# Weights' tiles of the first pass in the experts' buffers, loads three products ahead, and the second layer's first head among attention's last pieces

## The chip, the cores and the metric

The kernel runs on one core of a Trainium2 chip. The metric is the time of one execution in device microseconds; a kernel's time is the median of several executions. All tensors are float32. Engines are named as in the profile: PE is TensorE's matmul, PEld its weight load, DVE is VectorE, ACT is ScalarE, POOL is GpSimd and SP is SyncE, which here only issues DMAs. "SPq" is SP's sequencer.

## The reference

Two transformer layers run over 8 x 256 tokens of 512 channels. The reference, cut to what is computed:

```
x = hidden_states                      # 8 x 256 x 512
xn = layernorm(x)
x = x + attention0(xn) + ffn0(xn)      # layer 1
xn = layernorm(x)
x = x + attention1(xn) + ffn1(xn)      # layer 2

attention0: q, k, v = silu(xn @ qkv_w.T)             # 32 heads of 128
            o  = decayed causal linear attention of q, k, v
            o  = norm_w * o * rsqrt(mean(o*o) + eps) # over all heads
            return sigmoid(xn @ gate_w.T) * o @ out_w.T
ffn0:       16 experts, top 2 of them (inner size 128), and a shared expert
attention1: one head of 128: softmax(q k.T / sqrt(128)) v @ Wo + bo
ffn1:       G = softmax of the top 16 of 64 scores;  h[n,k,r] = xn @ A
            return 2 * sum over k, r of (h * G) * B  # rank 16
```

## The kernel before

**Attention of layer 1** takes most of the time. Its projections are made with the seven-product scheme of Strassen and Winograd, at two levels. The outer level cuts the tokens and a head group's weights in quarters, which gives seven weights' products, taken in the `ORDER` p1, p2, p6, p5, p3, p7, p4. The inner level cuts each of those again in seven, which run as `Outer`'s steps p1, p7, (the preceding product's p3), p6, p4, p2, p5 (L728, into the PSUM banks ps_a, ps_e, ps_b). The list `plan` holds 224 products: 2 passes over the tokens (`i`), 8 head groups (`g`), 2 halves (`h`: q and k, then gate and v), 7 weights' products. A "unit" in this document is one head group of one pass: two halves, 14 products.

**Weights** (`weights`, L664 to 714). A weights' tile holds eight blocks of 128x256: four blocks of the outer product's weight and four inner sums. In the first pass, p1, p2 and p4 (`RAW`) load 512 KB. p5, p6 and p7 load two raw quarters, 512 KB each, and DVE makes their outer sum in two instructions of 128x512 (`outer_sum`). p6 loads a third quarter into a buffer `st` and subtracts it, ACT copies p6's finished sum into `st` (L1051), and p3 subtracts `st` from its one quarter. Three of the inner sums are made by DVE and one by POOL (`inner_sum`, all recorded on line L103). ACT's queue then stores the sums in `ws`, from which the second pass loads them.

**Buffers.** `big` is a ring of four 1 MB tiles for weights, and later for other things of that size. `staged` is a pair of buffers, used by `st`, by the experts' tiles `xw` (second pass only), and by `spare8`. `toks` has three buffers for the tokens' operands `xt` (896 KB each, loaded at L423).

**The order of the work.** While product n runs, `prepare(n + 2)` makes the product two ahead: it issues its weights' load, and its sums are put among the products' steps (`following.step`). Smaller pieces of work wait in a list: `later(after, f)` queues a piece and `slot()`, called after each of the inner products, runs the next one due. Scores (L840), attended values (L852), the gated result gT (L872) and the output projection (L925, into ps_sc) are such pieces, as are the 36 experts, which run in the second pass. PE, DVE and SP are ordered by a scheduler within the limits of data and of `tc.keep_in_program_order`; ACT and POOL run in program order.

**Around the join of the layers.** `low_sums` (twice, near the end of the second pass) makes with POOL the sums of the operands `fa` and `fb` of ffn1 and stores them in `low` by SP (L1207; loads at L1211 and L1233). When a pass's attention is complete, `settle_sums` adds up each chunk's products: POOL combines them, DVE makes r (`finish`, L654), SP stores it in `xs`. `wrapped_up` loads chunk 0's sum, adds the experts' outputs and normalizes it. Then attention ends, the pool `toks` is closed (`layer1.close()`), and layer 2 loads its operands (`operands`, L1397 to 1402). It runs four chunks of 512 tokens: `Head` (values and routing scores L1441, `choose`'s gates L1446 to L1467, q and k L1430 and L1475, scores L1483, softmax), then the low-rank products (L1552 with A's operands `WA`, L1649 with B's operands `XB`), with the head of the next chunk beside the last of them. The gates go through DRAM (`gd`) and come back spread over partitions (`spread_g`, L1523).

Of the kernel before, what the change touches and what calls it, by code (L numbers as in the profile page):

```python
# [73 lines left out]
def block_kernel(  # L74
# [35 lines left out]
    layer1 = ExitStack()  # L110
    toks = layer1.enter_context(tc.tile_pool(name="toks", bufs=3))
# [307 lines left out]
    first_w = []  # L419
# [53 lines left out]
    for i in range(NCH):  # L473
# [8 lines left out]
        if i == 1:  # L482
            for p in ORDER[0:2]:
                w = big("w")
                nc.sync.dma_start(out=w[:, 0:4], in_=w_att[0, 0, RAW[p]])
                first_w.append(w)
# [121 lines left out]

    all_rms = {}
# [48 lines left out]

    def spare8():
        return staged("spare")[:, 0 : TPC * C].rearrange("p (t c) -> p t c", t=TPC)  # L660

    with tc.tile_pool(name="attn", bufs=1) as attn, tc.manual_schedule(engines={mybir.EngineType.Activation, mybir.EngineType.Pool}):
        sums_ = {}
        previous = {}  # L664
        finished = []

        def weights(i, g, h, p, steps):

            loaded = len(first_w) > 0
            w = first_w.pop(0) if loaded else big("w")  # L670
# [3 lines left out]
            kept = ws[2 * g + h][p]  # L674

            if i == 0:
                if not loaded:
                    tc.keep_in_program_order(nc.sync.dma_start(out=y, in_=w_att[g, h, dict(RAW, p6=2, p5=2, p3=1, p7=0)[p]]))
                outer = []
                if p in ("p6", "p5", "p7"):  # L680
                    tc.keep_in_program_order(nc.sync.dma_start(out=w[:, 4:8], in_=w_att[g, h, 2 if p == "p7" else 3]))
                    outer = [(sub if p == "p7" else add, w[:, 4:8])]
                if p == "p6":
                    previous["s2"] = staged("st")[:, 0 : 4 * S].rearrange("p (b n) -> p b n", b=4)
                    tc.keep_in_program_order(nc.sync.dma_start(out=previous["s2"], in_=w_att[g, h, 0]))
                    outer.append((sub, previous["s2"]))
                if p == "p3":
                    outer = [(sub, previous["s2"])]

                def outer_sum(n):  # L690
                    for f, other in outer:
                        f(y[:, n : n + 2], y[:, n : n + 2], other[:, n : n + 2], v)
# [9 lines left out]
                if outer:  # L702
                    steps += [("p4", partial(outer_sum, 0)), ("p2", partial(outer_sum, 2))]
                if p == "p6":
                    steps += [("p5", partial(nc.scalar.copy, previous["s2"], y))]
# [5 lines left out]
            elif p in RAW:  # L711
                tc.keep_in_program_order(nc.sync.dma_start(out=w[:, 1:4], in_=w_att[g, h, RAW[p]][:, 1:4]))
                tc.keep_in_program_order(nc.sync.dma_start(out=w[:, 4:8], in_=kept))
            else:
                tc.keep_in_program_order(nc.sync.dma_start(out=w[:, 1:8], in_=kept))
# [482 lines left out]
        def low_sums(n):  # L1198
# [7 lines left out]
            def store(at, t):  # L1206
                nc.sync.dma_start(out=low[n][:, at], in_=t)  # L1207
# [19 lines left out]
            def sums3():  # L1227
                if n == 0:
                    sub(t0[:, 1], t1[:, 1], t1[:, 0], pool)
                else:  # L1230
                    sub(t0[:, 1], t0[:, 1], t1[:, 1], pool)
                store(2, t0[:, 1])
                nc.sync.dma_start(out=t1[:, 0], in_=f[:, 1])  # L1233
# [9 lines left out]
        def wrapped_up():  # L1243

            x_, y = spare8(), spare8()
            nc.sync.dma_start(out=x_, in_=xs_[0])
# [25 lines left out]

        def prepare(n):
            if n < len(plan):
                outers.append(make(n))
            elif n == len(plan):
                nonlocal wsm
                wsm = big("wsm").rearrange("p b n -> p (b n)")
                load_small(wsm)
            else:  # L1280
                nonlocal yT0
                yT0 = big("yT0").rearrange("p (c b) n -> p c (b n)", c=NC)
                for t in range(TPC):
                    later(1 + 2 * t, lambda t=t: turn_rows(yT0, settled[0], t, ps_sc()))

        wsm = yT0 = None
        outers = [make(0), make(1)]
        for n, (i, g, h, p) in enumerate(plan):
# [4 lines left out]
            if k == 0:  # L1293
# [15 lines left out]
                if at == 2 * NB * NG - 2:  # L1309
                    later(1, wrapped_up)  # L1310
# [25 lines left out]
        outers[-1].p3()  # L1336
        while pieces:
            slot()
# [43 lines left out]
    layer1.close()  # L1382
    work = ctx.enter_context(tc.tile_pool(name="work2", bufs=2))
    wob = work.tile([P, 2, C], FP, tag="wob", name="wob", bufs=1)
# [3 lines left out]
    wqkv_t, bv_t, bqk_t = (small_part(wsm, n) for n in ("wqkv", "bv", "bqk"))  # L1388
# [16 lines left out]
    wa = operands(0, fa, "fa")  # L1405
    WA = dict(zip(("p1", "p2", "p4", "p7", "p5", "p6", "p3"), wa))
    xb = operands(1, fb, "fb")
    XB = dict(zip(("p1", "p2", "p3", "p7", "p5", "p6", "p4"), xb))
# [4 lines left out]
    def next_x(i):  # L1413
        x_ = spare8() if i % 2 == 0 else big(f"x{i}").rearrange("p (t b) n -> p t (b n)", t=TPC)
# [5 lines left out]
    scale = 1.0 / float(P) ** 0.5  # L1420
    out_t = out.rearrange("(i t p) c -> i t p c", t=TPC, p=P)
    class Head:


        def __init__(self, i):
            self.i, self.yT = i, xT[i]

        def project1(self, pm, w, lo):
            for c in range(NC):
                mm(pm, w[:, c, lo : lo + P], self.yT[:, c, :], start=(c == 0), stop=(c == NC - 1))  # L1430

        def route(self):

            self.v = work.tile([P, TPC, P], FP, tag="v", name="v1", bufs=1)
            sc = work.tile([P, TPC, K], FP, tag="sc", name="sc64", bufs=1)
            n = P + K
            for h in range(2):
                pv = ps_sc()
                for t in range(2 * h, 2 * h + 2):
                    for c in range(NC):  # L1440
                        mm(  # L1441
                            pv[:, bass.ts(t % 2, n)], self.yT[:, c, bass.ts(t, P)], wqkv_t[:, c, 2 * P :],
                            start=(c == 0), stop=(c == NC - 1),
                        )
                pv = pv[:, 0 : 2 * n].rearrange("p (t d) -> p t d", t=2)
                nc.vector.tensor_copy(sc[:, bass.ts(h, 2), :], pv[:, :, P:])  # L1446
                tt(self.v[:, bass.ts(h, 2), :], pv[:, :, 0:P], bv_t.to_broadcast([P, 2, P]), ALU.add)
            self.G = work.tile([P, TPC, K], FP, tag="gate", name="G", bufs=1)
            for t in range(TPC):
                top = work.tile([P, 8], FP, tag="top", name="top")  # L1450
                rest = work.tile([P, K], FP, tag="rest", name="rest")
                top2 = work.tile([P, 8], FP, tag="top2", name="top2")
                rest2 = work.tile([P, K], FP, tag="rest2", name="rest2")
                nm = work.tile([P, 1], FP, tag="nm", name="nm")
                es = work.tile([P, K], FP, tag="es", name="es")
                tot = work.tile([P, 1], FP, tag="tot", name="tot")
                nc.vector.max(top, sc[:, t, :])
                nc.vector.match_replace(rest, top, sc[:, t, :], NEVER)
                nc.vector.max(top2, rest)
                nc.vector.match_replace(rest2, top2, rest, NEVER)  # L1460
                nc.vector.tensor_scalar(nm, top[:, 0:1], -1.0, None, ALU.mult)
                nc.scalar.activation(es, sc[:, t, :], AF.Exp, bias=nm)
                nc.vector.scalar_tensor_tensor(
                    self.G[:, t, :], rest2, NEVER, es, ALU.is_equal, ALU.mult, accum_out=tot
                )
                nc.vector.reciprocal(tot, tot)
                nc.vector.tensor_scalar(self.G[:, t, :], self.G[:, t, :], tot, SCALING, ALU.mult, ALU.mult)  # L1467

        def qk(self):
            self.q = work.tile([P, CH], FP, tag="q", name="q1", bufs=1)  # L1470
            self.k = work.tile([P, CH], FP, tag="k", name="k1", bufs=1)
            for n, o in enumerate((self.q, self.k)):
                pm = ps_sc()
                self.project1(pm, wqkv_t, n * P)
                nc.scalar.activation(o, pm, AF.Identity, bias=bqk_t[:, n : n + 1])  # L1475

        def softmax(self):

            self.probs = []
            for b in range(2):  # L1480
                p = ps_sc()
                for t in range(2):
                    mm(  # L1483
                        p[:, bass.ts(t, S)], self.q[:, bass.ts(2 * b + t, P)], self.k[:, bass.ts(b, S)],
                        start=True, stop=True,
                    )
                pb = work.tile([P, 2, S], FP, tag="S", name="pb")
                top = work.tile([P, 2], FP, tag="stop", name="stop")
                tot = work.tile([P, 2], FP, tag="stot", name="stot")
# [270 lines left out]
```

## Time and profile before

| | us |
|---|---|
| median of 3 runs | 2806.41 |
| their lowest and highest | 2805.08, 2815.6 |
| the profiled execution's own time | 2803.46 |
| its span, first to last instruction | 2801.8 |
| busy in the span: PE, DVE, POOL, ACT | 2660.6, 1840.5, 1673.3, 973.8 |
| mean granted TensorE clock | 0.990 |

By place in the span, in us from its start: up to about 190 the first layer norm, routing and operands' sums; from there to about 1250 attention's first pass; from there to 2481 its second pass, with the experts; from 2481.0 (the first instruction of L1441) layer 2, with chunk 1's values at 2565.7 and the later chunks' at 2637.5 and 2709.9.

The profile is of one execution. A line of instructions gives the source line, the engine, the operation, the tiles by name as out<-in, shapes and a count, then busy time and the mean of one in nanoseconds, then idle time of the engine before them and what released it. A line of waits gives the engine and line that wait, an arrow to what they wait for, and then the sum in us, the number of waits and the longest. In brackets on a timeline stands the idle time before an instruction and its releaser.

### The profile page before, as it was taken

The page shows a single profiled execution, that of the slowest core. Times are in us where ns is not written, and L with a number is a line of the kernel's source. Part 1 is how long each engine was busy: PE and PEld are TensorE (multiplying, and loading weights), DVE is VectorE, ACT ScalarE, POOL GpSimd, SP SyncE. Part 2 cuts the span into 40 slices and gives each one's busy share as a digit, 9 for nine tenths or more (in the row PEclk, how much of TensorE's full clock was granted, in tenths as well). Part 3 has the DMA queues.
Part 4 walks back from the last instruction along what each step waited for, and adds up shares of the span by engine and source line. Part 5 has one row for each costly group of instructions (what it writes and reads, how often), then busy time and mean ns, then how long its engine had stood idle before and what let it go on. Part 6 is the DMA issues. An engine that isn't in the chain of part 4 may idle for free. (4 is left out here: it accounts for less than half of the span.)

```text
span 2801.8 us, 39316 instructions
## 1 busy us (share of the span) xinstructions
PE 2660.6 (95%) x14218; PEld 2297.3 (82%) x14218; DVE 1840.5 (66%) x3017; ACT 973.8 (35%) x1472; POOL 1673.3 (60%) x1484
## 2 busy tenths in 40 slices
PE   8989999899999999999999999999999999979999
PEld 5478888788887888888888888898989888957877
DVE  8688697979797878774535455555545455666663
ACT  4334343433343433343343324242323343521221
POOL 7367676767676767666755656565556666562210
PEclk9999999999999999999999999999999999989999
DMA  6898777868686868695768677776767586543211
GB/s 248 304 358 292 249 274 242 292 220 305 223 308 211 314 217 311 213 340 207 257 227 309 230 268 256 255 262 233 280 220 287 204 344 216 201 168 125 78 47 62
DMA packets 167011, 676.61 MB, mean 241 GB/s; under 512 B 20208, under 2 KB 22768, under 8 KB 164208
## 3 DMA queue, kind: packets, MB, share of 16 engines
q1 hardware_dynamic: 131264, 525.38, 53.3%
q10 hardware_dynamic: 21024, 92.81, 8.3%
q0 software_dynamic: 14528, 55.88, 6.3%
q8 instruction: 115, 1.88, 0.3%
q14 instruction: 80, 0.66, 0.1%
HBM read 531.00 MB, written 145.87 MB: 242 GB/s over the span
## 5 line engine op out<-in xcount | busy, mean ns | idle before, releaser
L728 PE MATMUL ps_a<-xt,w 128*128 128x256 f32 x2688 | 720.8, 383 | 35.1 <-DVE c L103 23.9
L103 POOL TENSOR_TENSOR c<-c,r 128x512 f32<-128x512 f32 x320 | 443.1, 1407 | 218.3 <-DVE r L103 214.7
L103 POOL TENSOR_TENSOR c<-c 128x512 f32<-128x512 f32 x288 | 372.7, 1315 | 323.1 <-DVE c L103 316.3
L728 PEld LDWEIGHTS ps_a<-xt,w 128*128 128x128 f32 x2688 | 469.1, 191 | 99.7 <-issue 22.2
L1055 ACT COPY cp<-ps_a 128x512 f32<-128x512 f32 x448 | 261.3, 584 | 747.8 <-PE ps_a L728 613.9
L925 PE MATMUL ps_sc<-wo,gT 128*128 128x256 f32 x1792 | 424.8, 381 | 19.4 <-DVE gT L872 18.7
L103 DVE TENSOR_TENSOR w<-w 128x256 f32<-128x256 f32 (+1 forms) x432 | 350.3, 827 | 106.7 <-DMA w<-in_w_att_dram 83.5
L728 PE MATMUL ps_e<-xt,w 128*128 128x256 f32 x1344 | 369.7, 383 | 21.3 <-DVE c L103 12.1
L925 PEld LDWEIGHTS ps_sc<-wo,gT 128*128 128x128 f32 x1792 | 332.8, 190 | 68.2 <-DVE gT L872 24.6
L103 POOL TENSOR_TENSOR sums<-sums,sq 128x256 f32<-128x256 f32 x240 | 192.0, 800 | 180.4 <-ACT sq L863 170.4
L728 PEld LDWEIGHTS ps_a<-w,xt 128*128 128x128 f32 x1792 | 271.0, 191 | 23.2
L728 PEld LDWEIGHTS ps_e<-xt,w 128*128 128x128 f32 x1344 | 233.2, 192 | 55.4 <-DVE c L103 14.5
L728 PE MATMUL ps_a<-w,xt 128*128 128x128 f32 x1792 | 272.6, 275 | 0.0
L103 DVE TENSOR_TENSOR acc<-ps_sc,acc 128x512 f32<-128x512 f32 x196 | 133.5, 686 | 146.9 <-PE ps_sc L925 145.0
L872 DVE SCALAR_TENSOR_TENSOR gT<-ps_o,nw,c 128x256 f32<-128x256 f32 x256 | 111.6, 477 | 167.6 <-ACT sq L863 160.4
L1055 ACT COPY cp<-ps_e 128x512 f32<-128x512 f32 x224 | 131.1, 585 | 155.1 <-PE ps_e L728 154.5
L728 PE MATMUL ps_b<-xt,w 128*128 128x256 f32 x672 | 182.2, 380 | 0.0
L103 POOL TENSOR_TENSOR gT<-gT 128x512 f32<-128x512 f32 x128 | 164.3, 1284 | 28.7 <-DVE gT L872 26.2
L103 DVE TENSOR_TENSOR s<-ps_sc,decay 128x384 f32<-128x384 f32 x256 | 139.8, 549 | 51.7 <-PE ps_sc L840 50.1
L103 DVE TENSOR_TENSOR c<-ps_a,c 128x512 f32<-128x512 f32 x160 | 109.5, 685 | 84.7 <-PE ps_a L728 76.5
L852 PE MATMUL ps_o<-s,c 128*128 128x256 f32 x512 | 154.9, 384 | 10.4 <-DVE gT L872 10.3
L863 ACT ACTIVATE sq<-ps_o 128x512 f32<-128x512 f32 x128 | 76.4, 597 | 253.2 <-PE ps_o L853 252.3
(291 smaller groups left out, 4398.4 us busy)
## 6 DMA issues: line engine op xcount, KB each, us to landing
xt<-xc SPq DMA_DIRECT2D x224, 896.0 KB
w<-in_w_att_dram SPq DMA_DIRECT2D x160, 512.0 KB
w<-in_w_att_dram SPq DMA_DIRECT2D x48, 384.0 KB
wo<-in_w_out_dram SPq DMA_DIRECT2D x56, 256.0 KB
decay<-dec SPq DMA_DIRECT2D x32, 384.0 KB
yd<-ye SPq DMA_DIRECT2D x36, 256.0 KB
st<-in_w_att_dram SPq DMA_DIRECT2D x16, 512.0 KB
wos<-wo ACTq DMA_DIRECT2D x32, 256.0 KB
```

The lines of the kernel that those rows point to most:

```text
L103: (eng or nc.vector).tensor_tensor(o, a, b, op)
L728: mm(o, a, b, start=(first and ty == 0), stop=True, skip_group_check=True)
L852: mm(po[:, bass.ts(hh, S)], v[:, 0:P], s[:, 0:S], start=True, stop=False)
L863: nc.scalar.activation(sq, po, AF.Square)
L872: nc.vector.scalar_tensor_tensor(gT[:, h, :], po[:, bass.ts(h, S)], nw[:, n : n + 1], self.c[:, 2 * h + t, 0:S], ALU.mult, ALU.mult,)
L925: mm(py[:, bass.ts(t, S)], self.O[l, p][:, hh, bass.ts(t, P)], self.wo[p][:, hh, :], start=(t == 0 and hh == 0), stop=(hh == 1), skip_grou ...
L1055: nc.scalar.copy(c, bank)
```

## The change

It has three parts, all in one diff.

1. **First pass, weights.** `load_weights` and `load_ahead` issue the loads three products ahead. The tiles of p5 and p7 lie in `staged`. p6 and p5 are loaded together, one quarter for p6 and two for p5. p5's outer sum w5 is made with p6's (w5 + its second quarter, then w5 - y for p6), p3 subtracts p6's sum itself; `st`, its load and ACT's copy are gone.
2. **Low sums.** The stores and one load of `low_sums` are issued from POOL's queue, the three first loads still from SP's. `wrapped_up` is queued 14 steps later in place of 1.
3. **Join.** The pool `toks` is kept. Nine of the fourteen 256 KB chunks of A's operands go to its three buffers during the last products (`load_part`), the other five after. The first head is made in pieces among attention's last ones, with its tiles in a `big` buffer. B's operands are loaded within chunk 0 (`load_fb`), and `next_x` exchanges its two kinds of buffers.

```diff
-    layer1 = ExitStack()
-    toks = layer1.enter_context(tc.tile_pool(name="toks", bufs=3))
+    toks = ctx.enter_context(tc.tile_pool(name="toks", bufs=3))
...
+    def load_part(n):
+
+        t = toks.tile([P, 7, S], FP, tag="X", name="fa")
+        load_fa(t.rearrange("p b n -> p (b n)")[:, 0 : 3 * C].rearrange("p (c k) -> p c k", c=3), 3 * n, 3 * n + 3)
...
+        def load_weights(i, g, h, p):
+
+            if i or p not in ("p5", "p7"):
+                w = big("w")
+            else:
+                w = staged("w")[:, 0 : 8 * S].rearrange("p (b n) -> p b n", b=8)
+            kept = ws[2 * g + h][p]
...
+            if i == 0:
+                load(w[:, 0:4], w_att[g, h, dict(RAW, p6=0, p5=2, p3=1, p7=0)[p]])
+                if p in ("p5", "p7"):
+                    load(w[:, 4:8], w_att[g, h, 2 if p == "p7" else 3])
...
-                if outer:
-                    steps += [("p4", partial(outer_sum, 0)), ("p2", partial(outer_sum, 2))]
+                outer = []
                 if p == "p6":
-                    steps += [("p5", partial(nc.scalar.copy, previous["s2"], y))]
+                    w5 = loaded["p5"][0]
+                    outer = [(add, w5, w5, w5[:, 4:8]), (sub, y, w5, y)]
+                elif p == "p3":
+                    outer = [(sub, y, y, latest["p6"])]
+                elif p == "p7":
+                    outer = [(sub, y, y, w[:, 4:8])]
+                for n, when in ((0, "p4"), (2, "p2")):
+                    steps += [(when, partial(outer_sum, *at, n)) for at in outer]
...
             def store(at, t):
-                nc.sync.dma_start(out=low[n][:, at], in_=t)
+                pool.dma_start(out=low[n][:, at], in_=t)
...
-                nc.sync.dma_start(out=t1[:, 0], in_=f[:, 1])
+                pool.dma_start(out=t1[:, 0], in_=f[:, 1])
...
+        def load(n):
+            if n < len(plan):
+                i, g, h, p = plan[n]
+                for q in dict(p6=("p6", "p5"), p5=()).get(p, (p,)) if i == 0 else (p,):
+                    loaded[q].append(load_weights(i, g, h, q))
+
+        def load_ahead(n):
+            if n + 1 < len(plan) and plan[n + 1][0] == 0:
+                load(n + 1)
+            elif n < len(plan) and plan[n][0]:
+                load(n)
+
         def prepare(n):
+            load_ahead(n)
             if n < len(plan):
                 outers.append(make(n))
             elif n == len(plan):
...
+                load_part(0)
             else:
-                nonlocal yT0
+                nonlocal yT0, head
+                load_part(1)
...
+                for n in range(2):
+                    later((10, 12)[n], partial(head.valued, n))
+                    later((14, 16)[n], partial(head.qk_, n))
+                for t in range(TPC):
+                    later(13 + t, partial(head.choose, (t,), attn))
+                later(22, partial(head.gates, lambda: attn.tile([P, 512], FP, tag="sum", name="GT", bufs=4)))
...
+                later(20, softened)
...
                 if at == 2 * NB * NG - 2:
-                    later(1, wrapped_up)
+                    later(14, wrapped_up)
...
-    head = Head(0)
-    head.route()
-    head.qk()
-    head.softmax()
...
+        if i == 0:
+            fill1[5].append(load_fb)
```

## The prediction

> **What bounds the kernel now.** I start from the page, to see which engine is nearly full and what its clock is.
>
> ```profile
> span 2801.8 us, 39316 instructions
> PE 2660.6 (95%) x14218; PEld 2297.3 (82%) x14218; DVE 1840.5 (66%) x3017; ACT 973.8 (35%) x1472; POOL 1673.3 (60%) x1484
> PEclk9999999999999999999999999999999999989999
> ```
>
> TensorE is busy 95% of the span, so the change, which leaves its products alone, can only win idle time: 2801.8 - 2660.6 = 141 us, and a little lost clock. The windows tell where it lies: columns are the stretch and its length, then busy time of PE, PEld, DVE, ACT, POOL, the granted clock, DMA share and GB/s.
>
> ```profile
> 490.00:630.00 140.00, 129.41 (x701) 113.66 (x699) 115.97 (x165) 52.06 (x75) 95.38 (x88) 1.00 0.74 256
> 1500.00:1640.00 140.00, 139.98 (x819) 125.32 (x818) 70.01 (x116) 46.10 (x72) 83.09 (x76) 1.00 0.72 252
> 2200.00:2300.00 100.00, 94.95 (x524) 84.89 (x523) 47.77 (x76) 31.36 (x48) 66.37 (x50) 1.00 0.76 287
> 2481.00:2520.00 39.00, 21.57 (x76) 14.73 (x76) 32.32 (x70) 6.03 (x17) 29.81 (x25) 0.78 0.73 262
> ```
>
> The first pass (row one) leaves PE idle 10.6 us in 140, with DVE 83% busy; the second pass (row two) leaves it idle for nothing. Row three is where the low-rank operands' sums are made: 5 us lost. Row four is the join of the layers: 17.4 us idle and the clock at 0.78. Next, in the first pass (200 to 1250 us, where PE is idle 70 us in all), who waits for whom:
>
> ```profile
> DVE w L103 <- DMA w<-in_w_att_dram: 83.4, 44, 4.4
> DVE gT L872 <- ACT sq L863: 38.6, 21, 2.8
> ...
> PE ps_sc L925 <- DVE gT L872: 17.4, 19, 1.6
> PE ps_a L728 <- DVE c L103: 16.9, 24, 1.5
> PE ps_e L728 <- DVE c L103: 12.1, 8, 3.2
> PE ps_o L852 <- DVE gT L872: 9.1, 7, 2.5
> PE ps_e L728 <- DVE r L103: 8.1, 14, 1.7
> ```
>
> PE waits for DVE's results, and DVE stands 83.4 us before weights that have not landed. A wait of DVE costs only where it makes a result late: going through PE's gaps one by one, 48 of the 70 us have a DVE wait for a DMA (or issue) in the 18 us before them. The sums' durations in that stretch, by form (busy us, mean ns, idle before):
>
> ```profile
> L103 DVE TENSOR_TENSOR w<-w 128x256 f32<-128x256 f32 x309 | 239.4, 789 | 62.2 <-DMA w<-in_w_att_dram 51.6 <-issue 4.2 <-POOL sums L103 2.5
> L103 DVE TENSOR_TENSOR w<-w 128x512 f32<-128x512 f32 x89 | 89.3, 1023 | 36.9 <-DMA w<-in_w_att_dram 28.4 <-issue 5.6 <-POOL c L103 2.3
> L103 DVE TENSOR_TENSOR w<-w,st 128x512 f32<-128x512 f32 x60 | 79.7, 1346 | 11.6 <-DMA w<-in_w_att_dram 3.5 <-ACT st L1051 2.7 <-DMA wos<-wo 2.6
> ```
>
> Last, the join, on PE's timeline (start, length, idle before) and SP's queue:
>
> ```profile
> 2481.01 5.45 PE L1441 MATMUL ps_sc<-wsm,yT 128*128 128x192 f32 x32
> 2486.29 3.60 PE L1430 MATMUL ps_sc<-yT,wsm 128*128 128x512 f32 x8
> 2497.64 5.43 PE L1430 MATMUL ps_sc<-yT,wsm 128*128 128x512 f32 x8 [7.75 <-DVE v L103]
> 2514.04 2.50 PE L1483 MATMUL ps_sc<-k,q 128*128 128x256 f32 x5 [9.68 <-ACT k L1475]
> SPq L1207 <- POOL low L103: 41.6, 7, 10.9
> ```
>
> The head's projections wait behind four r operations of DVE (8.79 us, then 4.94) and a G of 5.69; SP stands 41.6 us for POOL's low sums with loads behind it.
>
> **Part 1: weights.** Per half of a head group, loads fall from 5.5 to 4.5 MB, DVE sums of 128x512 by two, and ACT's copy of p6's raw sum (1.04 us) goes. Over 16 halves: 16 MB less, 32 sums x 1.02 to 1.35 = 33 to 43 us of DVE, 16.7 us of ACT (35% busy: worth nothing by itself). DVE's are worth only what they make PE wait less.
>
> In the issue order of the changed kernel each weight load stands one product earlier on SP, in front of the token load of the product before it. A product lasts 144.6/14 = 10.3 us (a unit, two halves, repeats every 144.6 us), the longest wait is 4.4 us, and each load's slot is free by its turn. So the 83.4 us of waits should go almost whole. That moves the token loads (L423) behind one more 0.5 or 1 MB transfer, 2 to 4 us at 256 GB/s; SP stood 934.9 us for their slots, each fetched two products ahead, so I cost it at nothing; uncovered, it would cost those 2 to 4 us a product.
>
> What does that win? I laid DVE's work by product, from row durations, against PE's (130.1 us per unit in both kernels) in the issue order of each kernel, without DMA waits. DVE has 120.4 us per unit before and 116.3 after. Before, that order alone gives about 6.0 us of PE stalls per unit, 3.7 of them in p1 of the first half, where gT and the results c stand behind sums. The trace has 9.1, so the waits cost at least 3.1 x 8 units = 25 us; the gap count says at most 48. I take 35, nearer the lower, since a gap near a wait need not come from it.
>
> But the sums are bunched in the new order. With p5's tile loaded beside p6's, p6, p5 and already p7 have their sums ahead of p1's gT and c: DVE's weight work in that product rises from 7.1 to 12.3 us, and its whole work from 11.8 to 17.1, while PE has 10.4. Five later products fall by 2 to 4 us each. By the same hand lay p1's stalls grow from 3.7 to 5.5 or 7, 2 to 3.3 us per unit: taken 3, x 8 = 25. Ends: 0 (a queue ahead has slack), and 5.3 x 8 = 42 (nothing hides). First pass: 35 - 25 = 10 us won; ends 48 won and 42 - 25 = 17 lost.
>
> A rule against this: POOL works beside, and the 128x256 sum takes 789 ns in the mean where its shortest is 406. The Trainium skill, "SBUF — State Buffer", section "SBUF: two separate sides", says that a VectorE operation with two SBUF inputs and a GpSimd operation share a port pair as a lock, the loser blocked for the whole of the other. By the rule at its worst each of the some six sums pulled forward would wait out one POOL c of 1.41 us, 8.4 instead of 5.3 us per unit; the traced mean, which holds the average wait, is what the sum uses.
>
> **Part 2: low sums' DMAs on POOL's queue.** SP's waits at L1207 go; the three DMAs that POOL waits for landed 3.9 to 5.9 us late, and PE lost 5 us in that window. POOL, 66% busy there, issues 10 more DMAs, by the nearest row (indirect DMAs of POOL, about 1.06 us) 10.6 us in 100. I take 4 us won; ends 5 won, 5 lost (if combines behind those issues came late). "DMA: Bandwidth & Descriptors", section "Latency and other measured facts", has GpSimd's first byte about 0.4 us later than SP's; for ten DMAs that would be an estimated 4 us, no run shows it, and it would eat this gain only if each were waited for.
>
> **Part 3: the head among attention's last pieces.** PE's work stays (32 products of 128x192 at 5.45 us, two times eight at some 3.6 to 5.4, scores 2.5): it lengthens the tail as much as it shortens the join. Won are the two stalls, 7.75 + 9.68 = 17.4 us, and part of the clock (0.78 in 39 us with 21.6 busy: at most 4.7). What comes in their place: the r operations (8.79 + 4.94) still run on DVE, now ahead of low_rank's sums and copies; the operands of fa are in toks' slots before that, except the last five chunks (1.25 MB, 5 us at 262 GB/s); the loads of fb go behind the r stores on SP, which left at 2497 and 2506. XB's first product came at 2547 before, so 30 us remain. Chunk 0 takes 84.7 us to the next head (2481.0 to 2565.7) where later chunks repeat every 72, and the gaps after the two stalls (2.12, 2.58, 0.51 us) I leave as they are. I take 15 won; ends 22 won, and 8 lost if one r block (8.79) with fb behind it stands in front of PE.
>
> **Sum.** 2803.46 (the profiled execution: span 2801.8 and 1.7 around it) - 10 - 4 - 15 = 2774.5. The median of the runs, 2806.41, is 3 us higher: 2777.
>
> **Rivals.**
> (a) The waits were the whole of it: all 48 us go, the bunch hides in queues, and with 15 + 4 the time is 2806 - 67 = 2739. For it: no other engine is over 83% there, and DVE's work falls. Against: 22 us of gaps have no DMA wait near.
> (b) The stalls only change their name: what the waits cost the bunch costs again. 2806 - 19 = 2787. For it: the lay gives nearly the same per unit.
> (c) Slower: the bunch in p1 is paid in full, 5.3 us x 8 = 42, and the cure is nothing, as DVE's lag was from its order. 2806 + 42 - 19 = 2829. It decides from 19/8 = 2.4 us lost net per unit, the size I expect of the bunch before the cure. Against: three later products of PE (13.9, 14.3, 13.9 us) have 2 to 6 us more than DVE and absorb the lag.
> (d) The loads don't come earlier after all, since DMA is 74% busy; then 32 fewer sums win perhaps 5 us: 2782, inside the forecast's range. Against: 2 MB less per unit.
>
> **How the numbers follow.** My forecast (2762 to 2792) has 0.42, (a) 0.20, (b) with weaker joins up to 2806 0.20, (c) and milder forms of it 0.18. A measurement can tell this kernel from no change from about 0.5%, 14 us: below 2792 is faster, above 2820 slower. Faster: 0.42 + 0.18 from (a) + 0.04 of (b) = 0.64. Same: 0.16 of (b) + 0.02 of (a)'s chance, where the joins take the gain back, + 0.02 of (c) = 0.20. Slower: 0.16. The range runs from near (a), 2742, to 2822, past the milder half of (c), and leaves out about 2 in 10.
>
> **What would show it.** Right: DVE's wait for in_w_att_dram in the first pass from 83 to under 10 us; PE idle there from 70 to about 60, more before gT of p1; SP's wait for low gone and its window at 99%; the 7.75 and 9.68 gaps gone, XB's p1 some 15 us earlier. Wrong: DMA waits stay (d); PE ps_sc <- gT and ps_a <- c above 60 us together (c); PE idle below 30 us in the first pass (a); a new wait of PE for fa or fb.

## The result, and the profile after

The changed kernel takes 2839.49 us in the median (2837.77 to 2841.13), against 2807.51 us before: a ratio of 1.0109, 95% interval 1.0087 to 1.013. It is slower, where faster by 29 us was forecast. The page of the profiled execution shows both halves of it: DVE's work fell by 52 us (33 to 43 had been counted), and PE's busy time rose by 15 us, though it has the same 14218 products.

```profile
PE 2675.2 (94%) x14218; PEld 2315.7 (82%) x14218; DVE 1788.3 (63%) x2985; ACT 958.2 (34%) x1455; POOL 1662.2 (59%) x1494
```

The place is found with marks that both kernels pass: 200 us, the first expert's transposes (1364.59 before, 1401.44 after), and the values of chunk 1 in layer 2 (2565.70 and 2602.55). The windows between them, before first and then after (PE, PEld, DVE, ACT, POOL, the granted clock, DMA share, GB/s):

```profile
200.00:1364.59 1164.59, 1087.09 (x5896) 958.84 (x5894) 910.45 (x1309) 436.41 (x631) 790.56 (x697) 1.00 0.75 263
1364.59:2565.70 1201.11, 1167.16 (x6596) 1036.20 (x6597) 644.84 (x1041) 419.33 (x640) 719.68 (x630) 0.99 0.69 245
```

```profile
200.00:1401.44 1201.44, 1098.57 (x5905) 974.95 (x5905) 856.53 (x1276) 421.44 (x616) 773.42 (x702) 0.98 0.67 243
1401.44:2602.55 1201.11, 1169.51 (x6596) 1039.74 (x6597) 643.90 (x1040) 420.72 (x640) 727.46 (x640) 0.99 0.69 244
```

The first pass is 36.85 us longer. PE's idle time in it rose from 77.5 to 102.9 us (window less busy: 25.4 more), and its busy time by 11.5 us at a clock of 0.98 in place of 1.00. Two small parts of these belong elsewhere: 2.6 us of the idle time is PE's wait for the first expert's own tile (4.13 us before, 6.69 after, and 0.92 to 8.04 in the runs below), and the window after holds nine more recorded matmuls, an estimated 2 us of busy time. The second pass with the join has the same 1201.11 us in both: what parts 2 and 3 were to win is not there.

The waits of the first pass (200 to 1290 us), in total, number and longest:

```profile
DVE w L103 <- DMA w<-in_w_att_dram: 85.3, 37, 4.5
...
PE ps_o L996 <- DVE gT L1016: 26.4, 7, 4.0
...
PE ps_sc L1069 <- DVE gT L1016: 14.5, 7, 2.5
```

DVE still waits for weights as long as before (83.4 us), and PE now waits 40.9 us for gT in 14 long waits, two a unit, where it had 26.5 us in 26 shorter ones. DVE's timeline ahead of one of them, and PE's beside it:

```profile
562.08 2.36 DVE L103 TENSOR_TENSOR w<-w 128x512 f32<-128x512 f32 x2
564.36 0.68 DVE L103 TENSOR_TENSOR acc<-ps_sc,acc 128x512 f32<-128x512 f32 x1
564.96 5.57 DVE L103 TENSOR_TENSOR w<-w 128x512 f32<-128x512 f32 x7
570.45 0.86 DVE L1016 SCALAR_TENSOR_TENSOR gT<-ps_o,nw,c 128x256 f32<-128x256 f32 x2
```

```profile
571.46 0.68 PE L996 MATMUL ps_o<-s,c 128*128 128x256 f32 x2 [3.99 <-DVE gT L1016]
```

Nine weights' sums for coming products, 7.93 us, stand ahead of the gT that PE needs now; no DMA wait is among them. In the same place of the kernel before, three sums of 4.02 us stand there behind a DMA wait of 0.21, and PE waits 1.21:

```profile
550.57 2.81 DVE L103 TENSOR_TENSOR w<-w 128x512 f32<-128x512 f32 x2 [0.21 <-DMA w<-in_w_att_dram]
553.31 1.21 DVE L103 TENSOR_TENSOR w<-w,st 128x512 f32<-128x512 f32 x1
555.45 0.67 PE L852 MATMUL ps_o<-s,c 128*128 128x256 f32 x2 [1.21 <-DVE gT L872]
```

Times below are in us; each ratio compares with the kernel before on the same chip, and the interval is the 95% one.

### The profile page after: what moved, and what is told of

It reads as the page before. It is cut to its first block, busy times and chain, and to the rows that moved or that the text cites. A ratio compares the mean times of both kernels' runs of the same rounds, so it can differ in the third digit from the quotient of the medians.

```text
span 2839.4 us, 39099 instructions
## 1 busy us (share of the span) xinstructions
PE 2675.2 (94%) x14218; PEld 2315.7 (82%) x14218; DVE 1788.3 (63%) x2985; ACT 958.2 (34%) x1455; POOL 1662.2 (59%) x1494
## 5 line engine op out<-in xcount | busy, mean ns | idle before, releaser
L103 POOL TENSOR_TENSOR c<-c,r 128x512 f32<-128x512 f32 x320 | 449.9, 1428 | 218.1 <-DVE r L103 216.4
L103 POOL TENSOR_TENSOR c<-c 128x512 f32<-128x512 f32 x288 | 362.6, 1281 | 350.6 <-DVE c L103 341.6
L872 PEld LDWEIGHTS ps_a<-xt,w 128*128 128x128 f32 x2688 | 474.9, 193 | 86.0 <-issue 28.7
L1069 PE MATMUL ps_sc<-wo,gT 128*128 128x256 f32 x1792 | 427.4, 383 | 15.6 <-DVE gT L1016 14.5
L103 DVE TENSOR_TENSOR w<-w 128x256 f32<-128x256 f32 (+1 forms) x464 | 366.7, 823 | 119.4 <-DMA w<-in_w_att_dram 92.1
L103 POOL TENSOR_TENSOR sums<-sums,sq 128x256 f32<-128x256 f32 x240 | 185.6, 773 | 230.5 <-ACT sq L1007 220.4
L872 PE MATMUL ps_b<-xt,w 128*128 128x256 f32 x672 | 188.1, 390 | 0.0
L996 PE MATMUL ps_o<-s,c 128*128 128x256 f32 x512 | 157.3, 389 | 26.5 <-DVE gT L1016 26.4
L983 PE MATMUL ps_sc<-c 128*128 128x256 f32 x512 | 156.3, 387 | 17.4 <-DVE s L103 11.9
```

Source lines behind the costliest of these rows:

```text
L103: (eng or nc.vector).tensor_tensor(o, a, b, op)
L872: mm(o, a, b, start=(first and ty == 0), stop=True, skip_group_check=True)
L983: mm(p[:, 0:S], k[:, 0:P], q, start=True, stop=True)
L996: mm(po[:, bass.ts(hh, S)], v[:, 0:P], s[:, 0:S], start=True, stop=False)
L1069: mm(py[:, bass.ts(t, S)], self.O[l, p][:, hh, bass.ts(t, P)], self.wo[p][:, hh, :], start=(t == 0 and hh == 0), stop=(hh == 1), skip_grou ...
```

## Experiments: which part costs the time

**Everything but the weights.** The changed kernel with before's `weights` and loads:

```diff
-        def load_weights(i, g, h, p):
...
-            load_ahead(n)
```

> The changed kernel with the weights of the first pass as before (loads two ahead, st and ACT's copy, p5 and p7 in the ring); low sums on POOL's queue and the join stay changed. Theory (the loss lies in the first pass, in the order of DVE's sums): the first expert's transposes come at 1364 us again as before (1401 after), and the time is within 5 us of before, about 2806. Rival (the join or the low sums cost the 37 us): it stays near 2839.

Measured: 2807.99, ratio 0.9995 (0.9982 to 1.0008). All of the loss is in the weights' part. The first expert comes at 1370.42; its DVE waits 91.8 us for weights in the first pass, more than the 83.4 before and the 85.3 after, and it loses nothing by that against before. The sum of those waits says nothing of the time.

**Loads two ahead.**

```diff
-            if n + 1 < len(plan) and plan[n + 1][0] == 0:
-                load(n + 1)
-            elif n < len(plan) and plan[n][0]:
+            if n < len(plan):
                 load(n)
```

> The changed kernel with its weights loaded two products ahead instead of three; nothing else. In its issue order DVE's weight work ahead of p1's results is 9.5 us, against 12.3 in the changed kernel and 7.1 before. Theory (bunched sums): about half of the loss goes, near 2822, and the gap before ps_o<-gT (3.3 to 4.0 us, once a unit) shrinks by half. Rival (the lead itself, by what it does to the token loads): all of the loss goes, 2806. Rival (lead is good, the tiles in the experts' buffers are bad): slower than 2839, as the waits for weights grow.

Measured: 2829.57, ratio 1.0067 (1.0042 to 1.0092): some 60% of the loss stays. The long wait before ps_o stays too (3.4 to 3.7 us once a unit), not halved; the one before ps_sc falls from 2.5 to at most 2.0 us.

**Sums pinned in program order**, with loads three and two ahead. DVE's sums may no longer be issued ahead of what stands before them in the program:

```diff
+                def pinned(f, o, a, b):
+                    tc.keep_in_program_order(v.tensor_tensor(o, a, b, ALU.add if f is add else ALU.subtract))
...
-                    f(o[:, n : n + 2], a[:, n : n + 2], b[:, n : n + 2], v)
+                    pinned(f, o[:, n : n + 2], a[:, n : n + 2], b[:, n : n + 2])
```

> The changed kernel with DVE's weights' sums held in program order, so that they can't be issued ahead of the results that stand before them in the program; loads three ahead. In its issue order the weight work in p1 falls from 12.3 to 2.4 us, and DVE falls behind PE by no more than 2.6 us anywhere. Theory (order): PE's waits for gT (41 us in the first pass) and DVE's waits for weights (85 us) both fall below 15, idle of PE from 94 to below 50 us between 200 and 1290, time 2775 to 2800. Rival (the loads or tiles cost it): 2830 to 2840, with the waits for weights as large as before.

> As the pinned kernel, with loads two products ahead: the same issue order on DVE and PE, so the difference is the lead of the loads alone. Theory (order is all, the sums now come late enough for either lead): within 5 us of the pinned kernel. Rival (the lead is what makes the weights land in time): DVE's waits for weights come back, 10 to 30 us slower than the pinned kernel.

Measured: 2809.34, ratio 1.0001 (0.9991 to 1.001), and 2807.84, ratio 1.0006 (0.9993 to 1.0019). The waits of the first pass, three ahead:

```profile
PE ps_a L878 <- DVE w L835: 32.0, 23, 2.0
...
PE ps_e L878 <- DVE w L835: 6.4, 7, 1.5
```

The loss is gone, and so are both waits, for landed weights and for gT: neither has a row left among the listed ones. But the time missed the forecast 2775 to 2800: PE is idle for 71.0 us of the 1090, where below 50 was forecast and 70.7 were before. It now waits 38.4 us for the weights' sums themselves, and 15.7 us more have no releaser that the profile shows. The sums had been issued too early and now come too late. The lead is worth nothing here.

**The same, one or two steps earlier in the program.**

```diff
-                for n, when in ((0, "p4"), (2, "p2")):
+                for n, when in ((0, "p6"), (2, "p4")):
...
-                        ("p2", (sub, 7, 1, 0)), ("p5", (add, 4, 0, 3)), ("1", (sub, 5, 4, 1)), ("2", (sub, 6, 2, 5))
+                        ("p2", (sub, 7, 1, 0)), ("p2", (add, 4, 0, 3)), ("p5", (sub, 5, 4, 1)), ("2", (sub, 6, 2, 5))
```

> The pinned kernel (loads three ahead) with its sums one or two steps earlier in the program: outer sums at p6 and p4 in place of p4 and p2, two inner sums one step earlier, still never ahead of the results before them. The pinned kernel's PE waited 38 us for the weights' sums themselves (23 and 7 waits of up to 2.0 us) and none for landed weights. Theory (there is a place between too early and too late): the 38 us fall by half or more, waits for gT stay small, time 2780 to 2795. Rival (DVE has too little room in the pass, a stall only moves from one result to another): 2800 to 2812.

> The same sums with loads two ahead. Theory (with sums this early the third product of lead is needed): DVE's waits for weights come back with some 20 to 60 us and the time is 5 to 20 us above the kernel with three ahead. Rival (lead is worth nothing at any place): equal within 3 us.

Measured: 2786.09, ratio 0.9912 (0.9892 to 0.9931), and 2785.97, ratio 0.9909 (0.989 to 0.9929). That is some 25 us faster than the kernel before and 53 us faster than the changed kernel, from which the first of the two differs in the order of DVE's sums alone. PE's idle time from 200 us to the first expert, now at 1343.96, is 52.4 us, against 77.5 before and 102.9 in the changed kernel. What is left of its waits for the sums:

```profile
PE ps_a L878 <- DVE w L835: 3.3, 6, 0.6
PE ps_e L878 <- DVE w L835: 3.1, 8, 0.4
```

PE's waits for the sums fall from 38.4 to 6.4 us, no wait for gT returns, and no wait for landed weights either. The third product of lead is again worth nothing.

**Only p7's outer sums pinned**, in the changed kernel:

```diff
-                    f(o[:, n : n + 2], a[:, n : n + 2], b[:, n : n + 2], v)
+                    (pinned if p == 'p7' else lambda f, o, a, b: f(o, a, b, v))(f, o[:, n : n + 2], a[:, n : n + 2], b[:, n : n + 2])
```

> The changed kernel with p7's outer sums alone held in program order, loads three ahead. DVE's weight work ahead of p1's results is 9.5 us in its issue order, as in the kernel with loads two ahead (2829.6), against 12.3 in the changed one (2839.5) and 7.1 before. Theory (time goes by the sums issued ahead of gT and c): 2822 to 2832. Rival (the two-ahead kernel was faster for its lead): 2839.

Measured: 2856.88, ratio 1.0174 (1.015 to 1.0198), slower than anything else and foreseen by neither theory. PE waits 47.6 us for gT (25.6 and 22.0), and DVE's longest wait for weights is 7.0 us. So the sum of weights' work ahead of p1's results doesn't order these kernels. What stands directly ahead of each gT explains the gaps that were read singly, whether that is work or a wait for a load: ahead of a gap of 3.37 us here (PE at 534.42), DVE waits 5.16 us for weights and then makes six sums in 3.05 us. How the 2.5 us gap of the changed kernel divides between the 3.38 us DMA wait shortly before it and the sums behind it, no run separates.

**The early pinned order on before's weights, and with before's join.** The first has the old sums, copy and loads; the second has the change's weights part alone:

```diff
-                    steps += [("p4", partial(outer_sum, 0)), ("p2", partial(outer_sum, 2))]
+                    steps += [("p6", partial(outer_sum, 0)), ("p4", partial(outer_sum, 2))]
```

> The kernel before (its loads, tiles and sums) with its sums pinned at the same early steps as in the fast pinned kernel (2786). Theory (what counts is where the sums stand; two sums and a copy fewer are worth little): 2786 to 2794. Rival (the 4 us per unit of DVE work that the change saves are needed, as DVE is 6.8 us behind PE at its worst in this order against 4.8): 2800 to 2812.

> The kernel before with the change's weights part alone, pinned at the early steps; low sums and join as before. Theory (the join gives at most 5 us): 2785 to 2793. Rival (the join is worth its 15 us here): 2800.

Measured: 2796.36, ratio 0.9952 (0.9937 to 0.9967), and 2787.24, ratio 0.9919 (0.9899 to 0.994). The order is worth 14 us to the kernel before, and the rest of the weights' part (32 sums, 16 copies and 16 MB of loads fewer, other tiles, the lead) some 9 us more once the order lets it. The traces place most of that: in the first, PE waits 10.0 us at ps_b for the sums (8 times), in the second not at all. The first missed its 2786 to 2794 narrowly, between its two theories. The second, without the changed join, is 1 us from the kernel with it (2786.09).

## Experiments: where the join's gain went

The head's pieces did fill attention's tail: the gaps of 7.75 and 9.68 us are gone. Three others of 19.0 us together came in chunk 0. The first is PE's, with DVE's timeline beside it:

```profile
2555.07 1.22 PE L1680 MATMUL ps_o<-pT,head 128*128 128x256 f32 x2 [8.96 <-DVE pT L1668]
```

```profile
2545.02 8.80 DVE L655 SCALAR_TENSOR_TENSOR r<-acc,rms,r 128x512 f32<-128x512 f32 x4 [2.23 <-POOL acc L103]
2553.74 0.68 DVE L103 TENSOR_TENSOR cp<-ps_b,cp 128x512 f32<-128x512 f32 x1
2554.34 1.27 DVE L1668 COPY pT<-ps_sc 128x512 f32<-128x512 f32 x2
2555.54 0.68 DVE L103 TENSOR_TENSOR cp<-ps_e,cp 128x512 f32<-128x512 f32 x1
2561.85 0.69 DVE L103 TENSOR_TENSOR hg<-cp,spread_g 128x512 f32<-128x512 f32 x1 [5.64 <-DMA spread_g<-gd]
```

The r block, 8.79 us in the kernel before and 8.80 here, stands ahead of the next thing PE needs in either place, and behind it DVE waits 5.64 us for the spread gates, three of whose four loads SP issued behind r's store (2553.84). The other two waits of PE are 3.96 (cp) and 6.11 (hg).

The block is not long by itself. Its four operations take 5.38, 2.17 and twice 0.74 us, and the other chunk's four, while POOL is idle, 2.74 us in all:

```profile
2543.70 6.14 POOL L103 TENSOR_TENSOR acc<-acc 128x512 f32<-128x512 f32 x5
2572.15 2.74 DVE L655 SCALAR_TENSOR_TENSOR r<-acc,rms,r 128x512 f32<-128x512 f32 x4
```

The operation of 5.38 us starts at 2545.02, within POOL's five adds, and ends 0.56 us behind the last of them. No run moved these adds, so that they hold DVE is a reading of the traces.

**The join without the low sums on POOL's queue**, and, of the fast pinned kernel, the same:

```diff
-                pool.dma_start(out=low[n][:, at], in_=t)
+                nc.sync.dma_start(out=low[n][:, at], in_=t)
```

> The kernel before with the join alone: weights as before and the low sums' DMAs back on SP's queue. Against the run with the low sums on POOL's queue (2808) it prices that part. Theory (the 4 us of the low sums are real): 2810 to 2813, with SP's wait for low (about 40 us) back. Rival (the loads behind them were not on the path): within 2 us of 2808.

> The fast pinned kernel (2786) with the low sums' DMAs back on SP's queue. The join alone ran 0.9981 of before with them there and 0.9995 with them on POOL's. Theory (POOL's queue costs some 4 us, since POOL's own waits for the loads stay and the indirect issues come on top): 2780 to 2784, ratio near 0.990. Rival (the two runs differed by chance): 2785 to 2788.

Measured: 2803.3, ratio 0.9981 (0.9963 to 0.9998), and 2783.27, ratio 0.9902 (0.9887 to 0.9917). By its interval the join alone wins between 0.5 and 10 us, some 5 by its middle. Both runs stand 3 to 5 us under their partners with POOL's queue, but the intervals overlap: the queue wins nothing, and that it costs is not shown. SP's wait for low is back (40.0 us) and costs nothing. The second is the fastest kernel here, 27 us under the kernel before.

**r behind the transposed probabilities and the first gates**, in the kernel with before's weights:

```diff
-            fill1[5].append(load_fb)
+            fill1[5].append(load_fb)
+            fill1[5] += behind[0:5]
+            fill1[4] += behind[5:]
```

> The kernel with before's weights (2808 us), and the last two chunks' r, their stores in xs and the second r's load issued inside chunk 0 of layer 2, behind the transposed probabilities and the first spread gates, in place of ahead of them. Theory (the join's 15 us were lost to r: PE waits 8.97 us for pT behind the r block, then 3.3 for cp and 5.7 for hg behind gates that SP fetches after r's store): the first two waits go and the third shrinks, 8 to 16 us faster than that kernel, 2792 to 2800. Rival (chunk 0 is bound by its own chain of gates and DVE): within 4 us of 2808.

Measured: 2810.43, ratio 1.0003 (0.9989 to 1.0016). Three waits (8.97, 3.3 and 5.7, 18 us) became one of 14.75 and two of 2.3 and 4.0. PE's line:

```profile
2538.46 2.08 PE L1630 MATMUL ps_e<-yT,fa 128*128 128x256 f32 x4 [14.75 <-DVE cp L103]
```

Ahead of cp, DVE waited 5.82 and 3.39 us for gates, then ran r in 7.76 us, now beside four adds of POOL (2530.41 to 2535.32).

**The first gates fetched ahead of the other loads**, on top of that:

```diff
+    gates0 = []
+    for h in range(2):
+        sp = work.tile([P, 2, CH], FP, tag="spread", name="spread_g")
...
+        gates0.append(sp)
...
-                gates2.extend(spread(h * HJ + j) for h in range(2))
+                gates2.extend(gates0 if i == 0 and j == 0 else [spread(h * HJ + j) for h in range(2)])
```

> The kernel with the late r (2810, before's weights) with chunk 0's first spread gates fetched ahead of the output projection's weights and of the last five chunks of A's operands, instead of behind them. Its PE stood 14.75 us before ps_e while DVE waited 5.8 and 3.4 us for spread gates and then ran r for 7.8. Theory (the join is held by the gates' way through DRAM and by r on DVE): the two waits for gates fall below 2 us together, the 14.75 falls to about 8, and the time is 5 to 8 us below that kernel, 2802 to 2805. Rival (the operands, now behind the gates, come late in their place): PE waits for fa and the time stays at 2810.

Measured: 2808.93, ratio 1.0004 (0.9988 to 1.0019). Two waits of PE, and a line of DVE's from ahead of the second:

```profile
2515.83 2.93 PE L1639 MATMUL ps_a<-ts,fa 128*128 128x256 f32 x6 [3.92 <-DMA fa<-low]
2537.39 2.93 PE L1639 MATMUL ps_e<-yT,fa 128*128 128x256 f32 x6 [8.20 <-DVE cp L103]
2530.24 6.50 DVE L630 SCALAR_TENSOR_TENSOR spare<-spare,slot_gates 128x512 f32<-128x512 f32 x2
```

The waits for gates go and the 14.75 falls to 8.20, as the theory had it; the operands that now stand behind the gates come 3.92 us late, as the rival had it; later waits (4.07 before fbs) take the rest. But r is not what stands ahead of cp here: it takes 2.73 us. The time beside POOL's adds fell on others, 6.48 us on one hg (five adds, 2509.94 to 2516.07) and 6.50 on two operations on `spare` that take 1.40 elsewhere (four adds from 2530.61). So the join is held by several things of nearly one length: the gates through DRAM, the operands' loads, and whichever operation of DVE meets POOL's adds. Taking away one or two of them won nothing; all of them, or the adds, were not tried.

## Why the prediction was wrong, point by point

1. **"So the 83.4 us of waits should go almost whole"** is the step that failed. The loads did move a product forward on SP. But the sums moved forward with them (nine against three ahead of the gT shown above), and the waits stayed (85.3). DVE's order is a scheduler's; that it puts a sum where it reckons the weights to have landed fits this, but no run shows its reckoning. I compared the loads' new places with the old places of the sums. The pinned kernels show the two apart: with the sums held, no such wait is left and the loss is gone, with the same loads and tiles and at either lead.
2. **The cure of 35 us** was therefore nothing. That 48 of 70 us of gaps had a DMA wait of DVE ahead of them did not make the waits their cause: the pinned kernel has no such wait and is idle as long (71.0 us), now for the sums.
3. **The bunch, taken as 25 us,** was nearly exact in idle time (25.4 us more), though the hand lay put it all in p1, and it lies in front of two gTs. That the number agrees is in part luck: the same lay gave the kernel with p7's sums pinned less work there (9.5 us against 12.3), and that kernel lost more. Missing was the term that long gaps cost clock, most of the 11.5 us more of busy time. The cure (35), the clock (11.5), the join (15) and the low sums (4) together make 65.5 us; the profiled execution missed the sum by 66.6 (2841.13 against 2774.5).
4. **The join, 15 us:** about 0 in the changed kernel, some 5 in the run of the join alone. The mechanism of the low end ("one r block (8.79) with fb behind it stands in front of PE") is in the main what happened, with the gates' loads in place of fb's; it took the gain and not 8 us more. I had subtracted the old gaps and not laid out the chain that ends after them, and I took r at its 8.79 us without asking what it ran beside.
5. **The low sums, 4 us:** nothing. SP's wait was not in front of anything PE needed; POOL's own waits for the loads went only from 14.9 to 10.9 us. The sign named for it, that window at 99%, did not come: in the same 100 us (2236.85 to 2336.85 in the changed kernel) PE is idle for 7.3 us, against 5.0 before.
6. **The rivals.** (c) had the mechanism, 42 us of bunch, and its sign, but was given 0.18 and spared 19 us for the other parts; the first pass took 36.9, near that end. Held against it was that three later products of PE absorb DVE's lag; that does not help a gT for which PE waits now. That DVE's work falls, which spoke for (a), was beside the matter too: the order decided. The prediction itself quoted that order, 17.1 us of DVE's work against 10.4 of PE's in p1.
7. **The marks** misled in one place. "DMA waits stay" was to mean (d), that the loads don't come earlier; they stayed though the loads did. The mark of (c), ps_sc <- gT and ps_a <- c above 60 us, did not show: the waits stood at ps_o <- gT (26.4) and at ps_sc <- gT (14.5).

## What to carry to other kernels

Where a scheduler orders an engine, moving a load forward can move the work that it releases too, and that work then stands in front of results another engine needs now; ask for the new place of the work, not of the load alone. Holding such work back has its price as well (2839 floating, 2809 held, 2786 placed a step or two earlier), so place it by hand and read which wait remains. A gap at the join of two stages is worth only what the next chain leaves: here each wait that was taken away came back in another place. And before working around a long operation, ask whether it is long by itself or by what runs beside it.

## What the runs showed of the hardware

Gaps of PE cost clock as well as their length. In the changed kernel's first pass (200 to 1290 us), all 16 gaps of 1.3 to 1.6 us left the clock at 1.00 in the 6 us from the gap's start. Of 18 gaps of 2.19 to 4.00 us, 12 were followed by 0.72 to 0.95 in that stretch, and six of 2.28 to 2.45 us by 1.00. Length alone doesn't decide: in the kernel before, a gap of 3.19 us (to 495.53) was followed by 1.00. Two windows, the first over the end of the gap of 3.99 us, the second behind it:

```profile
570.00:572.00 2.00, 0.54 (x3) 0.52 (x4) 2.00 (x6) 0.00 (x0) 0.61 (x1) 1.00 0.76 213
572.00:576.00 4.00, 4.00 (x14) 3.41 (x13) 3.96 (x6) 2.12 (x4) 2.82 (x4) 0.57 0.13 53
```

The Trainium skill, "TensorE: Matmul & The Clock Gate", section "HAM oscillation — how this bites in real kernels", sets the limit at idle gaps of about 3.4 us. Here the measurement decides: gaps of 2.19 to 2.46 us were followed by a lowered clock in five cases out of eleven.

In the join, an operation of DVE that meets a run of POOL's adds ends behind the whole run, not behind one add: the r of 5.38 us and the hg of 6.48 us above, of the same shape as operations of 0.68 to 0.74 us, both end 0.56 us behind a run of five. The prediction let such an operation wait out one of POOL's (1.41 us). In both places the two come together; no run took the adds away.
